# Attention and scan on one core: where the weighted sums stand in the slot order, and how the input norm is computed

## The chip, the cores and the metric

The kernel runs on one core of a Trainium2 chip. The metric is device time in microseconds; before the change it is 6852.26 us, the median of 3 runs (6847.03 to 6880.9). All arithmetic is float32.

## The reference, cut to what matters

Two layers are added to `x` (8 batches, 1024 tokens, 512 channels) one after the other. The change touches the first, an attention whose weights are modulated by a style vector per batch:

```python
x = x * s1[:, None, :]                       # s1 = cond[:, :512]
mu = jnp.mean(x, axis=-1, keepdims=True)
var = jnp.mean(jnp.square(x - mu), axis=-1, keepdims=True)
x = (x - mu) * jax.lax.rsqrt(var + EPS_IN)   # the input norm
q = heads(einsum('bsh,oh->bso', x, q_weight) * q_dc)      # 16 heads of 32
k = heads(einsum('bsh,oh->bso', x, k_weight) * k_dc)
v_flat = einsum('bsh,oh->bso', x, v_weight) * v_dc * s2
attn = softmax(einsum('bhqd,bhkd->bhqk', q, k) * scale)
out = einsum('bhqk,bhkd->bhqd', attn, heads(v_flat))      # the weighted sums
out = einsum('bsh,oh->bso', out, w_weight) * w_dc
skip = einsum('bsh,oh->bso', v_flat, u_weight) * u_dc
return out + skip
```

The factors `q_dc` to `u_dc` ("demodulation") are one over the root of sums of squared weights times squared styles. The second layer, a gated scan over the tokens, follows in the same program and isn't changed.

## The kernel before, in words

The order of instructions on every engine is the order in which the program writes them; no scheduler moves them. The attention is a loop over **slots**. A block is a batch `b` and a group `o` of four heads (128 channels); a block has 16 slots: 8 query tiles of 128 tokens (`q`), each with two pairs of heads (`pair`). So there are 32 blocks and 512 slots, and the loop index `n` counts slots (L302).

A slot does the following for its two heads, and overlaps it with the slot before:

- `scores` (L226): four matmuls on quarters of the array, 32 rows each, into two score tiles of two PSUM banks each. Two such tiles exist, so the next slot's scores need this slot's exps to be done.
- VectorE takes the row maxima from PSUM (L327), ScalarE the exps with their sums (L336), VectorE the reciprocals (L341, L354), and GpSimd (POOL) scales the probabilities in place (L356).
- The probabilities of the slot before are flipped by `flip` (L241, eight transposes a head on TensorE). Each flip of four tiles is copied out of PSUM into `pT`, by ScalarE (L333, L347) and VectorE (L338, L346).
- Two slots (four heads) share one `pT`. `weigh` (L248) multiplies it with the transposed values `vt`, in columns of 32, into the PSUM tile `av`. Before the change this runs in two halves of 16 matmuls, at the ends of the two slots that follow (L352), and VectorE copies `av` to `aT` one slot later (L319).

Work of other blocks is fed in as **background**: `background` (L275) is a generator of pieces, each some instructions long. A slot runs some of its pieces between the first and the second flips (L342) and the rest at its end (L357). `PIECES` (L298) gives the number of pieces of a block by `o`, spread evenly. Pieces are: `project` (L150), chains of four matmuls of 512 columns that make q, k and v of the next block, two matmuls to a piece, with an evacuation in the second piece by ScalarE (L165, L169, L174), then two pieces of four transposes of v (L182); `out_u` and `out_w`, chains with evacuation by VectorE (L198, L214); and `norm` of the next batch, whose first half is done in `o=2` and whose second in `o=3`. All of these chains share one PSUM buffer, `ps_m` (L95).

`norm` (L113) works on channels by tokens: GpSimd multiplies by the style (L116), a chain with a matrix of 1/512 gives the mean in every partition, VectorE subtracts it (L121), GpSimd squares (L127), a second chain gives the variance, ScalarE takes the root (L132), VectorE the reciprocal (L136), GpSimd multiplies (L140). A half is 512 tokens, 4 tiles of 128 channels. `load_x` (L56) fetches a half from `xT`, ahead of its use.

Before the loop, in program order: both halves of batch 0 are loaded, the five weight matrices are loaded (two buffers) and squared, and small matmuls make the demodulation factors (L64 to L87); then both halves are normed, the first weights fetched, and block 0 projected.

Of the kernel before, what the change touches and what calls it, by code (L numbers as in the profile page):

```python
# [28 lines left out]


@with_exitstack
def modulated_attention(ctx, tc, const, x1_d, xu_d, S, xT, wT, ident, sT):

# [7 lines left out]
    nc = tc.nc  # L41
    HW = S // 2
    KT = S // P
# [7 lines left out]
    ones = const.tile([P, P], F32, name="ones_h")  # L51
    nc.vector.memset(ones, 1.0 / H)
    dc = const.tile([P, 5, KH, B], F32, name="dc")
    xp = ctx.enter_context(tc.tile_pool(name="xh", bufs=3))

    def load_x(b, hf):  # L56
        xh = xp.tile([P, KH, HW], F32, name="xh")
        nc.sync.dma_start(
            out=xh, in_=xT[b, :, hf * HW : (hf + 1) * HW].rearrange("(k p) t -> p k t", p=P)
        )  # L60
        return xh

    xh_now = [load_x(0, 0), load_x(0, 1)]
    with tc.tile_pool(name="w0", bufs=2) as wp, tc.tile_pool(name="ps_d", bufs=2, space=PSUM) as ps_d:  # L64
# [27 lines left out]
    small = ctx.enter_context(tc.tile_pool(name="small", bufs=6))  # L92
    ps_s = ctx.enter_context(tc.tile_pool(name="ps_s", bufs=2, space=PSUM))
    ps_t = ctx.enter_context(tc.tile_pool(name="ps_t", bufs=2, space=PSUM))
    ps_m = ctx.enter_context(tc.tile_pool(name="ps_m", bufs=1, space=PSUM))  # L95
    ps_v = ctx.enter_context(tc.tile_pool(name="ps_v", bufs=1, space=PSUM))

    def half(hf):
# [4 lines left out]
    def chain(pieces, evac):  # L103

        ps = ps_m.tile([P, HW], F32, tag="mm", name="mm_ps")
        for k, (w, x) in enumerate(pieces):
            nc.tensor.matmul(ps, w, x, start=(k == 0), stop=(k == KH - 1))  # L107
            if k == 1:
                yield
        evac(ps)  # L110
        yield

    def norm(xh, b):  # L113

        for k in range(KH):
            nc.gpsimd.tensor_scalar(xh[:, k], xh[:, k], sT[:, k, b : b + 1], 1.0, ALU.mult, ALU.mult)  # L116
        yield

        def center(ps):
            for k in range(KH):  # L120
                nc.vector.tensor_sub(xh[:, k], xh[:, k], ps)  # L121

        yield from chain([(ones, xh[:, k]) for k in range(KH)], center)
        sq = []
        for k in range(KH):
            sq.append(ring.tile([P, HW], F32, tag="sq", bufs=4, name="sq"))
            nc.gpsimd.tensor_mul(sq[k], xh[:, k], xh[:, k])  # L127
        yield
        rstd = ring.tile([P, HW], F32, tag="rstd", bufs=1, name="rstd")
        yield from chain(  # L130
            [(ones, sq[k]) for k in range(KH)],
            lambda ps: nc.scalar.activation(rstd, ps, AF.Sqrt, bias=eps),  # L132
        )
        for k in range(KH):
            c = slice(k * P, (k + 1) * P)
            nc.vector.reciprocal(rstd[:, c], rstd[:, c])  # L136
            if k % 2 == 1:
                yield
        for k in range(KH):
            nc.gpsimd.tensor_mul(xh[:, k], xh[:, k], rstd)  # L140
        yield

    def load_w(name, o):
# [101 lines left out]
            nc.tensor.transpose(ps[:, j], pr[:, c0 : c0 + P], ident)  # L245
        return ps

    def weigh(av, pT, vt, part):  # L248
        for kt in range(4 * part, 4 * part + 4):
            for i in range(4):  # L250
                r = slice(i * HD, (i + 1) * HD)
                nc.tensor.matmul(  # L252
                    av[r], vt[:, kt, r], pT[:, i, kt], start=(kt == 0), stop=(kt == KT - 1),
                    skip_group_check=True,
                )

    blocks = [(b, o) for b in range(B) for o in range(KH)]
    sts = {bo: {} for bo in blocks}
    slots = [(bo, q, pair) for bo in blocks for q in range(NQ) for pair in range(2)]
# [15 lines left out]
    def background(n):  # L275

        nonlocal xh_now
        b, o = blocks[n]
        if o == 2 and b + 1 < B:
            xh_next.append(load_x(b + 1, 0))  # L280
        if o < KH - 1:
            yield from project(wts[n + 1], xh_now, b, o + 1, sts[b, o + 1])
            if o == 2 and b + 1 < B:
                xh_next.append(load_x(b + 1, 1))
                yield from norm(xh_next[0], b + 1)
        elif b + 1 < B:
            yield from norm(xh_next[1], b + 1)
# [9 lines left out]
    xh_next = []  # L297
    PIECES = {0: 22, 1: 22, 2: 23, 3: 39}  # L298
    probs = None
    flipped = {}  # L300
    bg, ran = iter(()), 0
    for n in range(len(slots) + 4):  # L302
        bo, q, pair = slots[n] if n < len(slots) else (None, None, None)
        if n % SB == 0:
            for _ in bg:
# [5 lines left out]
            ran += due  # L311


        m = (n - 5) // 2
        if n % 2 == 1 and m >= 0:
            mbo, mq, _ = slots[2 * m]
            if mq == 0:
                sts[mbo]["a"] = ring.tile([P, S], F32, tag="aT", bufs=6, name="aT")
            nc.vector.tensor_copy(sts[mbo]["a"][:, mq * P : (mq + 1) * P], flipped.pop(m)[1])  # L319
        fresh = None  # L320
        if bo is not None:
            s_ps = scores(sts[bo], q, pair)
# [4 lines left out]
                nc.vector.tensor_reduce(nmax[i], s_ps[i], AX.X, ALU.max, negate=True)  # L327
        if probs is not None:
            if (n - 1) % 2 == 0:
                flipped[(n - 1) // 2] = [two.tile([P, 4, KT, P], F32, name="pT"), None]  # L330
            pT = flipped[(n - 1) // 2][0][:, 2 * ((n - 1) % 2) : 2 * ((n - 1) % 2) + 2]
# [12 lines left out]
        if probs is not None:  # L344
            t_ps = [flip(probs[1], g) for g in range(2)]
            nc.vector.tensor_copy(pT[:, 1, 4:8], t_ps[1])  # L346
            nc.scalar.copy(pT[:, 1, 0:4], t_ps[0])  # L347
# [478 lines left out]
def network(ctx: ExitStack, tc: tile.TileContext, S, ins, out):  # L826
    nc = tc.nc
    const = ctx.enter_context(tc.tile_pool(name="const", bufs=1))
# [6 lines left out]
    nc.sync.dma_start(out=sT, in_=ins["condT"].rearrange("(k p) b -> p k b", p=P))  # L835
    with tc.manual_schedule():
        modulated_attention(
            tc, const, x1_d, xu_d, S, ins["xT"], {n: ins[f"w{n}T"] for n in "qkvwu"}, ident, sT
        )
# [68 lines left out]
```

## Time and profile before

| | |
|---|---|
| median of 3 runs | 6852.26 us (6847.03 to 6880.9) |
| the profiled execution | 6840.93 us |
| its span, first to last instruction | 6838.9 us |
| mean granted clock of TensorE | 0.947 |
| first scores of the attention | 117.1 us |
| last scores of the attention | about 3695 us |
| TensorE busy, of the stretch 0 to 4000 us | 3662 us |
| VectorE, ScalarE, GpSimd busy there | 2358, 2096, 1334 us |

Times in the profile are microseconds from the start of the span. "PE" is TensorE's matmuls and "PEld" its weight loads, which overlap them; DVE is VectorE, ACT is ScalarE, POOL is GpSimd, SP the engine that issues the DMAs. A row of a timeline gives the start, the length, the engine, the source line, the operation, and the tile written with those read. A float32 matmul other than a transpose shows as two records. The attention is regular: blocks with the same `o` take the same time in batches 1 to 6.

### The profile page before, as it was taken

To read this page: it belongs to the slowest core of one execution; us is meant where nothing else is said; L and a number is where in the kernel's file an instruction comes from. 1 tells how busy PE (TensorE), PEld (TensorE's weight loads), DVE (VectorE), ACT (ScalarE), POOL (GpSimd) and SP (SyncE) were. 2 spreads that over 40 slices of the span, in tenths; PEclk is the share of its full clock that TensorE was granted. 3 is DMA by queue.
4 is the path that set the end of the run, shared out by engine and by line. 5 is a ranking of instruction groups with operands and counts; after the bars stand their busy time and mean duration, and the time that the engine had idled before them with its cause. 6 is when DMAs were issued, how large, how long until landed. Compare 5 with 4: busy or idle time off the path is not lost.

```text
span 6838.9 us, 113125 instructions
## 1 busy us (share of the span) xinstructions
PE 6072.8 (89%) x42960; PEld 3291.8 (48%) x42960; DVE 4499.3 (66%) x6851; ACT 3919.7 (57%) x6713; POOL 1333.6 (20%) x1220
## 2 busy tenths in 40 slices
PE   7889989899899898998997788888888888888887
PEld 4555545555555455555554444444434444444443
DVE  2656656656566566565664677777777777777776
ACT  3555545545555455555553566666666666666665
POOL 2343333423433334234332000000000000000000
PEclk9999999999999999999999898999889998899898
DMA  2011111111111111111112777778777787777776
GB/s 67 18 32 50 46 43 41 30 55 44 33 49 46 43 44 29 57 43 37 44 34 75 192 202 202 199 197 208 202 196 204 199 209 200 196 203 196 202 205 174
DMA packets 493518, 777.47 MB, mean 114 GB/s; under 512 B 197008, under 2 KB 295448, under 8 KB 492976
## 3 DMA queue, kind: packets, MB, share of 16 engines
q1 hardware_dynamic: 492976, 770.22, 43.3%
q8 instruction: 342, 5.60, 0.3%
q14 instruction: 200, 1.64, 0.1%
HBM read 659.40 MB, written 83.89 MB: 109 GB/s over the span
## 4 chain that ended last, share of the span: by engine, by line
PE 64%; DVE 17%; DMA 7%; ACT 4%; issue 4%; SPq 2%; POOL 1%; DVEq 0%; ACTq 0%; POOLq 0%
PE mm_ps L107 17%; PE t_ps L245 12%; PE s_ps L235 7%; PE av L252 7%; DVE h L755 7%; PE o_ps L701 5%; PE g_ps L663 4%; DMA xb<-xd 4%; PE y_ps L742 3%; PE in_ps L508 3%; DVE nmax L327 2%; PE p_ps L539 2%; SPq L724 1%; ACT xb L731 1%; DVE gate L678 1%
## 5 line engine op out<-in xcount | busy, mean ns | idle before, releaser
L755 DVE CUSTOM_DVE_ANT_0 h<-h,xb,lim 128x1024 f32<-128x1024 f32 x1024 | 1374.1, 1342 | 587.5 <-ACT xb L731 335.2
L327 DVE TENSOR_REDUCE nmax<-s_ps 128x1 f32<-128x1024 f32 x1024 | 1205.0, 1218 | 767.6 <-PE s_ps L238 763.7
L356 POOL TENSOR_SCALAR pr<-pr,rinv 128x1024 f32<-128x1024 f32 x1024 | 1148.2, 1122 | 2279.5 <-PE t_ps L245 1515.8
L245 PEld LDWEIGHTS t_ps<-ident,pr 128*128 128x128 f32 x8192 | 904.7, 141 | 868.1 <-issue 609.0
L245 PE MATMUL t_ps<-ident,pr 128*128 128x128 f32 x8192 | 1156.7, 280 | 170.3 <-DVE pT L338 124.8
L336 ACT ACTIVATE pr<-s_ps,nmax 128x1024 f32<-128x1024 f32 x1024 | 1141.5, 1115 | 83.9 <-DVE nmax L327 60.3
L731 ACT ACTIVATE xb<-xb,ws 128x1024 f32<-128x1024 f32 x1024 | 1154.0, 1140 | 30.8 <-DMA xb<-xd 30.8
L333 ACT COPY pT<-t_ps 128x512 f32<-128x512 f32 x512 | 300.1, 586 | 1313.6 <-PE t_ps L245 1313.6
L742 PE MATMUL y_ps<-h,yw 128*32 128x512 f32 x4096 | 647.1, 720 | 8.0 <-DVE h L755 8.0
L346 DVE COPY pT<-t_ps 128x512 f32<-128x512 f32 x512 | 353.2, 690 | 399.9 <-PE t_ps L245 397.7
L235 PE MATMUL s_ps<-kT,qT 32*128 32x512 f32 x2048 | 579.7, 640 | 0.0
L238 PE MATMUL s_ps<-k,q 32*128 32x512 f32 x2048 | 577.1, 640 | 0.0
L252 PE MATMUL av<-pT,vt 128*32 128x128 f32 x16384 | 559.2, 278 | 0.4 <-DVE aT L319 0.4
L508 PE MATMUL in_ps<-x,win 128*128 128x256 f32 x2048 | 543.2, 412 | 3.6 <-DMA x<-x_d 2.8
L508 PEld LDWEIGHTS in_ps<-x,win 128*128 128x128 f32 x2048 | 401.2, 205 | 162.8 <-issue 59.2
L701 PE MATMUL o_ps<-wout,gT 128*128 128x512 f32 x1024 | 468.0, 600 | 0.5 <-ACT gT L689 0.5
L252 PEld LDWEIGHTS av<-pT,vt 128*32 128x32 f32 x16384 | 420.1, 110 | 88.0 <-issue 86.6
L663 PE MATMUL g_ps<-win,x1t 128*128 128x512 f32 x1024 | 460.5, 592 | 0.4 <-ACT x1t L658 0.4
L527 DVE SCALAR_TENSOR_TENSOR xc<-xr,cw,xc 128x256 f32<-128x256 f32 x768 | 370.7, 483 | 26.7 <-ACT xc L520 8.4
L338 DVE COPY pT<-t_ps 128x512 f32<-128x512 f32 x512 | 348.4, 680 | 2.6 <-PE t_ps L245 2.6
L347 ACT COPY pT<-t_ps 128x512 f32<-128x512 f32 x512 | 297.4, 581 | 82.2 <-PE t_ps L245 82.2
L684 PE MATMUL gt_ps<-ident,gate 128*128 128x128 f32 x512 | 108.8, 350 | 243.7 <-DVE gate L678 243.7
(128 smaller groups left out, 6381.5 us busy)
## 6 DMA issues: line engine op xcount, KB each, us to landing
xb<-xd SPq DMA_DIRECT2D x2048, 256.0 KB
xd<-xt SPq DMA_DIRECT2D x64, 512.0 KB
xh<-in_xT SPq DMA_DIRECT2D x16, 1024.0 KB
q<-qT SPq DMA_DIRECT2D x128, 128.0 KB
xr<-in_xT SPq DMA_DIRECT2D x64, 256.0 KB
xu_d<-xr SPq DMA_DIRECT2D x64, 256.0 KB
xr<-xu_d SPq DMA_DIRECT2D x64, 256.0 KB
x_d<-xr SPq DMA_DIRECT2D x64, 256.0 KB
```

The costliest lines, as they stand in the source:

```text
L107: nc.tensor.matmul(ps, w, x, start=(k == 0), stop=(k == KH - 1))
L235: nc.tensor.matmul(s_ps[i][:, 0:HW], st["q"][r, qc], st["k"][r, 0:HW], start=True, stop=True)
L245: nc.tensor.transpose(ps[:, j], pr[:, c0 : c0 + P], ident)
L252: nc.tensor.matmul(av[r], vt[:, kt, r], pT[:, i, kt], start=(kt == 0), stop=(kt == KT - 1), skip_group_check=True,)
L327: nc.vector.tensor_reduce(nmax[i], s_ps[i], AX.X, ALU.max, negate=True)
L336: nc.scalar.activation(fresh[i], s_ps[i], AF.Exp, bias=nmax[i], accum_out=rsum[i])
L356: nc.gpsimd.tensor_scalar(fresh[i], fresh[i], rinv[i], 1.0, ALU.mult, ALU.mult)
L508: nc.tensor.matmul(ps, win_sb[:, kk, k * P : (k + 1) * P], st["x1"][:, kk].rearrange("p b t -> p (b t)"), start=(kk == 0), stop=False,)
L701: nc.tensor.matmul(ps, st["gT", i][:, k, :], wout_sb[:, k, :], start=False, stop=(k == KI - 1), skip_group_check=True,)
L731: nc.scalar.mul(xbs[n], xbs[n], sts[c]["ws"][:, t : t + 1])
L742: nc.tensor.matmul(st["y", i][32 * r : 32 * r + 32, hf * 512 : (hf + 1) * 512], yws[i][:, 4 * q + r, :], hs[4 * g + r][:, hf * 512 : (hf + ...
L755: nc.vector._custom_dve(dve_ops.TENSOR_ADD_SAT, out=h, in0=last["h"], in1=xbs.pop(n), s0=lim[:, 0, t : t + 1], s1=lim[:, 1, t : t + 1],)
```

## The change

It has three parts. First, `weigh` runs whole, 32 matmuls, in every second slot (odd `n`), ahead of that slot's scores; the copy of `av` to `aT` follows at once, and the loop has two slots fewer at its end. Second, `norm` works on tokens by channels: `x` is loaded by tokens, with the style spread over 128 partitions by the DMA; GpSimd multiplies by the style, VectorE takes mean and variance with `bn_stats` and `bn_aggr`, ScalarE the root of the 128x4 variances, GpSimd scales and shifts, and TensorE transposes the result into `xh`, four 128x128 tiles into a PSUM bank at a time, evacuated in turn by ScalarE and VectorE. A half is now 10 pieces where it was 9, and `PIECES` follows. Third, batch 0 is normed before the demodulation, whose matmuls now use the shared PSUM buffer.

```diff
     def load_x(b, hf):
+        xq = tok.tile([P, 4, H], F32, name="xq")
+        nc.sync.dma_start(
+            out=xq, in_=x[b, hf * HW : (hf + 1) * HW].rearrange("(j p) c -> p j c", p=P)
+        )
+        sr = tok.tile([P, H], F32, name="sr")
+        nc.sync.dma_start(out=sr, in_=cond[b, 0:H].unsqueeze(0).to_broadcast([P, H]))
+        return xq, sr
+
+    def norm(xs, put):
+        xq, sr = xs
         xh = xp.tile([P, KH, HW], F32, name="xh")
-        nc.sync.dma_start(
-            out=xh, in_=xT[b, :, hf * HW : (hf + 1) * HW].rearrange("(k p) t -> p k t", p=P)
-        )
-        return xh
-
-    xh_now = [load_x(0, 0), load_x(0, 1)]
+        put(xh)
+        mv = small.tile([P, 4, 2], F32, name="mv")
+        rs = small.tile([P, 4, 2], F32, name="rs")
+        for j in range(4):
+            nc.gpsimd.tensor_mul(xq[:, j], xq[:, j], sr)
+            if j % 2 == 1:
+                yield
+        for j in range(4):
+            stat = small.tile([P, 6], F32, name="stat")
+            nc.vector.bn_stats(stat, xq[:, j])
+            nc.vector.bn_aggr(mv[:, j], stat)
+            if j % 2 == 1:
+                yield
+        nc.scalar.activation(rs[:, :, 0], mv[:, :, 1], AF.Sqrt, bias=eps)
+        nc.vector.reciprocal(rs[:, :, 0], rs[:, :, 0])
+        nc.vector.scalar_tensor_tensor(
+            rs[:, :, 1], mv[:, :, 0], -1.0, rs[:, :, 0], ALU.mult, ALU.mult
+        )
+        yield
+        for j in range(4):
+            nc.gpsimd.tensor_scalar(xq[:, j], xq[:, j], rs[:, j, 0:1], rs[:, j, 1:2], ALU.mult, ALU.add)
+        yield
+        for k in range(KH):
+            ps = ps_m.tile([P, 4, P], F32, tag="mm", name="mm_ps")
+            for j in range(4):
+                nc.tensor.transpose(ps[:, j], xq[:, j, k * P : (k + 1) * P], ident)
+            if k % 2 == 0:
+                nc.scalar.copy(xh[:, k], ps.rearrange("p j t -> p (j t)"))
+            else:
+                nc.vector.tensor_copy(xh[:, k], ps.rearrange("p j t -> p (j t)"))
+            yield
+
+    xh_now = []
+    first = [load_x(0, 0), load_x(0, 1)]
+    for xs in first:
+        for _ in norm(xs, xh_now.append):
+            pass
...
-            d_ps = ps_d.tile([P, KH, B], F32, name="d_ps")
+            d_ps = ps_m.tile([P, KH, B], F32, tag="mm", name="mm_ps")
...
-    for hf in range(2):
-        for _ in norm(xh_now[hf], 0):
-            pass
...
-    def weigh(av, pT, vt, part):
-        for kt in range(4 * part, 4 * part + 4):
+    def weigh(av, pT, vt):
+        for kt in range(KT):
...
-    PIECES = {0: 22, 1: 22, 2: 23, 3: 39}
+    PIECES = {0: 22, 1: 22, 2: 24, 3: 40}
...
-    for n in range(len(slots) + 4):
+    for n in range(len(slots) + 2):
...
-        m = (n - 5) // 2
+        m = (n - 3) // 2
         if n % 2 == 1 and m >= 0:
             mbo, mq, _ = slots[2 * m]
+            av = ps_v.tile([P, P], F32, name="av")
+            weigh(av, flipped.pop(m), sts[mbo]["vt"])
             if mq == 0:
                 sts[mbo]["a"] = ring.tile([P, S], F32, tag="aT", bufs=6, name="aT")
-            nc.vector.tensor_copy(sts[mbo]["a"][:, mq * P : (mq + 1) * P], flipped.pop(m)[1])
+            nc.vector.tensor_copy(sts[mbo]["a"][:, mq * P : (mq + 1) * P], av)
...
-        m = (n - 3) // 2
-        if 0 <= m < len(slots) // 2:
-            if n % 2 == 1:
-                flipped[m][1] = ps_v.tile([P, P], F32, name="av")
-            weigh(flipped[m][1], flipped[m][0], sts[slots[2 * m][0]]["vt"], (n + 1) % 2)
```

The old `norm` goes out whole, with the matrix of 1/512. In `background` the loads of the next batch stay where they were; only the tiles that they hand over are others.

More of the change, by code (lines that the diff above doesn't have):

```diff
@@ L31, in modulated_attention @@
 @with_exitstack
-def modulated_attention(ctx, tc, const, x1_d, xu_d, S, xT, wT, ident, sT):
+def modulated_attention(ctx, tc, const, x1_d, xu_d, S, x, xT, cond, wT, ident, sT):
     nc = tc.nc
@@ L50, in modulated_attention @@
     nc.vector.memset(eps, EPS)
-    ones = const.tile([P, P], F32, name="ones_h")
-    nc.vector.memset(ones, 1.0 / H)
     dc = const.tile([P, 5, KH, B], F32, name="dc")
     xp = ctx.enter_context(tc.tile_pool(name="xh", bufs=3))
+    tok = ctx.enter_context(tc.tile_pool(name="tok", bufs=2))
+    small = ctx.enter_context(tc.tile_pool(name="small", bufs=6))
+    ps_m = ctx.enter_context(tc.tile_pool(name="ps_m", bufs=1, space=PSUM))
     def load_x(b, hf):
-        xh = xp.tile([P, KH, HW], F32, name="xh")
-        nc.sync.dma_start(
-            out=xh, in_=xT[b, :, hf * HW : (hf + 1) * HW].rearrange("(k p) t -> p k t", p=P)
-        )
-        return xh
@@ L63, in modulated_attention @@
-    xh_now = [load_x(0, 0), load_x(0, 1)]
-    with tc.tile_pool(name="w0", bufs=2) as wp, tc.tile_pool(name="ps_d", bufs=2, space=PSUM) as ps_d:
+        xq = tok.tile([P, 4, H], F32, name="xq")
[7 more added lines that the diff above has]
+        xq, sr = xs
+        xh = xp.tile([P, KH, HW], F32, name="xh")
+        put(xh)
[15 more added lines that the diff above has]
+            rs[:, :, 1], mv[:, :, 0], -1.0, rs[:, :, 0], ALU.mult, ALU.mult
+        )
+        yield
[11 more added lines that the diff above has]
+            yield
@@ L65, in modulated_attention @@
+    xh_now = []
[3 more added lines that the diff above has]
+            pass
+    with tc.tile_pool(name="w0", bufs=2) as wp:
         s2T = wp.tile([P, 2 * KH, B], F32, name="s2T")
@@ L91, in modulated_attention @@
     pp = ctx.enter_context(tc.tile_pool(name="pp", bufs=4))
-    small = ctx.enter_context(tc.tile_pool(name="small", bufs=6))
     ps_s = ctx.enter_context(tc.tile_pool(name="ps_s", bufs=2, space=PSUM))
     ps_t = ctx.enter_context(tc.tile_pool(name="ps_t", bufs=2, space=PSUM))
-    ps_m = ctx.enter_context(tc.tile_pool(name="ps_m", bufs=1, space=PSUM))
     ps_v = ctx.enter_context(tc.tile_pool(name="ps_v", bufs=1, space=PSUM))
@@ L110, in chain @@
         evac(ps)
[L111 to L132, printed above, removed]
-        )
[L134 to L140, printed above, removed]
         yield
@@ L279, in background @@
         if o == 2 and b + 1 < B:
-            xh_next.append(load_x(b + 1, 0))
+            todo.append(load_x(b + 1, 0))
         if o < KH - 1:
@@ L283, in background @@
             if o == 2 and b + 1 < B:
-                xh_next.append(load_x(b + 1, 1))
-                yield from norm(xh_next[0], b + 1)
+                todo.append(load_x(b + 1, 1))
+                yield from norm(todo.pop(0), xh_next.append)
         elif b + 1 < B:
-            yield from norm(xh_next[1], b + 1)
+            yield from norm(todo.pop(0), xh_next.append)
             xh_now = list(xh_next)
@@ L295, in background @@
             yield from out_u(b, [sts[b, k]["v"] for k in range(KH)])
-    xh_next = []
-    PIECES = {0: 22, 1: 22, 2: 23, 3: 39}
+    todo, xh_next = [], []
+    PIECES = {0: 22, 1: 22, 2: 24, 3: 40}
     probs = None
@@ L329, in modulated_attention @@
             if (n - 1) % 2 == 0:
-                flipped[(n - 1) // 2] = [two.tile([P, 4, KT, P], F32, name="pT"), None]
-            pT = flipped[(n - 1) // 2][0][:, 2 * ((n - 1) % 2) : 2 * ((n - 1) % 2) + 2]
+                flipped[(n - 1) // 2] = two.tile([P, 4, KT, P], F32, name="pT")
+            pT = flipped[(n - 1) // 2][:, 2 * ((n - 1) % 2) : 2 * ((n - 1) % 2) + 2]
             t_ps = [flip(probs[0], g) for g in range(2)]
@@ L837, in network @@
         modulated_attention(
-            tc, const, x1_d, xu_d, S, ins["xT"], {n: ins[f"w{n}T"] for n in "qkvwu"}, ident, sT
+            tc, const, x1_d, xu_d, S, ins["x"], ins["xT"], ins["cond"], {n: ins[f"w{n}T"] for n in "qkvwu"}, ident, sT
         )
@@ L869 @@
     arrays = {
+        "x": np.asarray(x),
         "xT": np.asarray(x).transpose(0, 2, 1),
```

## The prediction

> **What bounds the kernel now.** First the page: the parts with the engines and with the chain that ended last.
>
> ```profile
> PE 6072.8 (89%) x42960; PEld 3291.8 (48%) x42960; DVE 4499.3 (66%) x6851; ACT 3919.7 (57%) x6713; POOL 1333.6 (20%) x1220
> PE 64%; DVE 17%; DMA 7%; ACT 4%; issue 4%; SPq 2%; POOL 1%; DVEq 0%; ACTq 0%; POOLq 0%
> ```
>
> The matmuls of the attention (the first 3,730 us) carry the chain, so I need the order on TensorE, not the busy sums. The timeline of one slot gives it (start, length, engine; the bracket is the idle time before and what ended it):
>
> ```profile
> 1500.37 0.19 PEld L235 LDWEIGHTS s_ps<-kT,qT 32*128 32x128 f32 x2 [0.20 <-issue]
> 1501.44 0.86 PEld L245 LDWEIGHTS t_ps<-ident,pr 128*128 128x128 f32 x8 [0.76 <-issue]
> ...
> 1505.03 0.19 ACT L336 ACTIVATION_READ_ACCUMULATOR pr<-s_ps,nmax 128x1 f32 x1
> 1505.16 0.81 PEld L252 LDWEIGHTS av<-pT,vt 128*32 128x32 f32 x32 [0.17 <-issue]
> 1505.69 0.58 ACT L347 COPY pT<-t_ps 128x512 f32<-128x512 f32 x1
> 1506.17 0.30 PEld L107 LDWEIGHTS mm_ps<-xh,w_k 128*128 128x128 f32 x2 [0.20 <-issue]
> 1508.08 0.19 PEld L235 LDWEIGHTS s_ps<-kT,qT 32*128 32x128 f32 x2 [0.76 <-issue]
> ```
>
> The slot reads: scores S 1.07 us; first flips F0 0.83; background piece B1 1.40; second flips F1 with what follows 1.49, so that the sums W start at S+4.79; W 1.01, ending at 5.80; background B2 1.91. With B2 a slot is 7.71, without it 5.80. ScalarE ends the second exp at S+4.75, then evacuates B1 if due (0.68), then makes the last copy of the flips (L347) at S+4.74 to 5.32, or here, behind an evacuation, to 5.90.
>
> The first slots have no sums yet, so they show how slots run once W is gone:
>
> ```profile
> 126.83 0.23 PEld L235 LDWEIGHTS s_ps<-kT,qT 32*128 32x128 f32 x2 [0.17 <-ACT pr L336]
> 132.34 0.30 PEld L107 LDWEIGHTS mm_ps<-xh,w_v 128*128 128x128 f32 x2 [0.86 <-ACT kT L169]
> ```
>
> Scores then wait for the exp of the slot before; a B2 that begins a chain just after a B1 that ended one waits 0.86 us for the single mm_ps buffer.
>
> Stretches of 10 us around the norm (TensorE, its weight loads, DVE, ACT, POOL busy; then the clock):
>
> ```profile
> 1310.00:1320.00 10.00, 7.16 (x88) 4.36 (x76) 7.89 (x14) 6.69 (x11) 2.81 (x4) 1.00 0.00 0
> 1320.00:1330.00 10.00, 6.19 (x62) 3.63 (x61) 6.37 (x10) 5.84 (x11) 10.00 (x11) 1.00 0.01 2
> 1330.00:1340.00 10.00, 7.09 (x67) 4.05 (x66) 6.37 (x11) 3.16 (x7) 6.62 (x7) 1.00 0.01 2
> 1340.00:1350.00 10.00, 10.00 (x108) 5.59 (x107) 3.78 (x6) 5.66 (x10) 3.36 (x3) 1.00 0.00 0
> 1350.00:1360.00 10.00, 4.91 (x52) 3.36 (x48) 8.05 (x13) 5.30 (x9) 6.70 (x6) 0.76 0.01 2
> ```
>
> Here TensorE idles about 15 us per batch. Starts of scores give block times (16 slots): 103.0 for o=0 and 1, 104.7 for o=2, 143.1 for o=3, the same in batches 1 to 6.
>
> [...] a weight load waits 0.76 us from a 512-column chain into scores, 0.24 from chain to chain; 0.17 before W, 0.20 behind it. [...] the trace has 0.76 at 1350 to 1360, after stalls in which only flips ran. [...] a switch loads a table; the trace agrees, at 1.28 us a load [...].
>
> **The sums moved.** Two times 16 matmuls become 32 in one place: 1.01 + 1.01 becomes about 1.83 (the tail has 32 beside each other, 64 records in 1.9). Each pair of slots loses one entry (0.17) and one exit (0.20), and where an even slot has B2, W comes behind it, at the price of the drain that scores paid there (0.76 - 0.24 = 0.52). But W now comes at the start of an odd slot, directly behind F1 of the even slot, whose last copy (L347) it reads from its fourth matmul on; in the old place it read the slot before. So:
> - even slot without B2: W resumes at S+5.37, slot 7.15; with an evacuation ahead of L347 7.73.
> - even slot with B2 (it hides L347): 4.62 + 1.40 + 0.5 drain + 1.83 = 8.36; if B2 waits 0.89 for mm_ps, which W used to hide: 9.25.
> - odd slot without B2: scores follow F1, at the end of the second exp, 4.85. With B2 6.53; if that waits 7.42.
>
> Queued behind the waiting W are the next scores, and behind them reductions, exps and POOL. The aT copy sits ahead of the reductions on DVE but ends (0.29) under the 1.07 of scores: nothing.
>
> A block o=0 or 1 (22 pieces, B2 in slots 0, 2, 5, 8, 10, 13), pairs after minus before: (0,1) 13.21-13.51 = -0.30; (2,3) 14.10-13.51 = +0.59; (4,5) 14.57-13.51 = +1.06; (6,7) 12.58-11.60 = +0.98; (8,9), v's transposes, 12.80-12.20 = +0.60; (10,11) -0.30; (12,13) 13.68-13.51 = +0.17; (14,15) +0.40. Sum +3.2; x14 = +45. In batch 0 the pieces end early: +4.1 twice.
>
> **The norm.** Removed per half: 8 chain matmuls of 0.854 (6.8 us of TensorE), 4 subtractions 0.68, 4 reciprocals 0.914, POOL 4 each of 0.70, 1.04 and 1.27. Added: 16 transposes (4 take about 0.43 of issue), four evacuations 0.58 (ACT) or 0.69 (DVE), 4 bn_stats at 0.69 and 4 bn_aggr at 0.21 (rows of the second stage[...]), POOL 4 at 1.27 and 4 at 0.70. The two table loads per half stay. No row shows POOL's scaling with two columns; bounds 0.56 (half of the 1.12 of L356) and 1.27, I take 0.70. The x load grows by 0.25 MB of broadcast styles; DMA share is 0.1 to 0.2: nothing.
>
> Walk of o=2 (24 pieces): slots 0 to 7, all even ones with B2, 54.6; 8 and 9 12.7; then slot 10 7.1, 11 4.9, 12 9.45 (sqrt and its table load at S+5.6 to 7.05 delay L347 to 7.6, W waits), 13 6.1 (exp table reload), 14 7.5, 15 4.9. Sum 107.3 against 104.7: +2.6, x8 = +21.
> o=3 (40 pieces): slot 0 7.2 (POOL's four products, 5.1, push the first scaling of pr to 8.35, just in time), slot 1 4.9, slot 2 10.4 (the first transposes wait for POOL's four scalings, ready at S+6.1, almost 4 us of idle TensorE), slot 3 6.05: 28.5 against 39.0. Slots 4 to 15, by the prices above, 105.1 against 104.1. Sum -9.5, x7 = -66. Batch 7, without norm, +1.5.
>
> **The clock.** Before has one half-clock episode a batch, worth about 2.3 us (W 1.94 for 1.08, flips, one chain), inside the 143.1. After has two candidate stalls (o=2 slot 12, o=3 slot 2), none in my walk. I add one episode a batch, +16; none would be 0, two +32.
>
> **The start.** Before: demodulation ends at 51.3, the norm takes until 88.3 on the path, scores at 117.1. After: x at about 7.5 (SP issues x and styles ahead of w, so w lands some 0.5 MB later than 12.7, long before its turn); per half POOL 5.1, stats and roots 1.9, scalings 2.8, four transposes with evacuations 5.6; POOL's in-order halves end with scalings at 27.3, transposes at 33. ScalarE squares the weights only behind that, so d_ps starts at 34, takes 36.5 (the two w buffers gate it as before; d_ps in one PSUM buffer adds some 0.2 each, under the wait for w) to 70.5, w_q lands about 74, and 28.8 later scores start at 103: -14 (-8 to -18). The end loses two slots of sums: -1.
>
> Sum: 45 + 8 + 21 - 66 + 1.5 + 16 - 14 - 1 = +10 on a profiled 6840.9 us, of which the span is 6838.9. The median shown is 6852.3, 11 higher; I put the sum on it: **6862**.
>
> **Rivals.**
> A, faster: the newly exposed waits don't appear, because W's first matmuls and the reordered loads cover L347, or the mm_ps waits close. For: the order on TensorE really loses a drain in every pair. Against: 1505.69 for L347 lies behind 1505.16. Without these waits a block o=0 or 1 is 5.5 better (-88), the others about 2 each: about 6745; with half of it, 6805. 0.13.
> B, slower: ScalarE's loop becomes the bound of odd slots. It holds 0.59 + 2.34 + 0.19 + 0.58 + 0.68 = 4.4 of the 4.85 us that I give them, and scores there wait for the second exp; the early instance took 5.0. Some 165 odd slots have no B2. At 0.15 more each it adds 25 and passes the bound of 34 us together with my sum; at 0.4, 66: about 6920. For: the wait on L336 in the early slot. Against: that slot had unevenly started scores. 0.30 with all that lies above 6886.
> C, the norm's gain comes larger: POOL's scalings at 0.56, no clock episode, DVE free earlier: 6862 - 16 - 7 x 2 = 6832. Inside no change.
> D, the kernel is the same but for the start: gains and losses cancel otherwise: 6838. It lies inside no change too; C and D have 0.25 of its 0.57.
>
> **How the numbers follow.** About 0.5% (34 us) is what a measurement of this kernel can tell from no change. Faster (A) 0.13, within 0.57, slower (B, and two clock episodes with slow norm stalls) 0.30. The error of a pair, about 0.1 us over 256 pairs, is 26; the norm walk 3 a batch, 21; start 6. The range that leaves out 0.2 is 6815 to 6910: at the low end half of A, at the high end most of B.
>
> **What would show it.** Right: scores from slot to slot alternate near 7.15 or 8.36 and 4.85; L347 becomes the releaser of W in even slots without B2 (0.5 to 1.1 us each, some 64 of them in o=0 and 1); waits of mm_ps behind qT, kT, vT grow; block times about 106, 106, 107, 134; first scores near 103. Wrong: no wait of W on L347 (A); odd slots at 5.2 or more (B); block o=3 not under 138 (the norm still stalls); first scores not before 110; two stretches of low clock a batch.

## The result, and the profile after

The changed kernel takes 6896.4 us (median of 13 runs, 6877.1 to 6916.9) where the kernel before took 6851.2 (13 runs, 6838.6 to 6880.9): a ratio of 1.0053, interval 1.0037 to 1.0068. It is slower by 45 us in the medians (0.66%) and by 0.53% in the ratio, just beyond the 0.5% that I called "no change". The forecast was +10, with a range that holds the result. The profiled execution took 6894.9 us, its span 6893.1, against 6840.9 and 6838.9: +54.

The page of the changed kernel, with the parts on the engines and on the chain that ended last:

```profile
PE 6051.7 (88%) x42960; PEld 3345.8 (49%) x42960; DVE 4490.3 (65%) x6914; ACT 3925.7 (57%) x6744; POOL 1272.4 (18%) x1156
PE 54%; DVE 19%; ACT 11%; DMA 9%; issue 4%; SPq 2%; POOL 0%; DVEq 0%; ACTq 0%; POOLq 0%
```

TensorE has 21 us less work than before and the kernel is longer: work is not what grew. The chain has moved in part from TensorE (54%, it was 64%) to ScalarE (11%, it was 4%). The timeline at the end of an even slot without B2 (block o=1 of batch 3; its scores start at 1622.67) and the first scores of the odd slot behind it say where (start, length, engine, line; the bracket is the idle time before and what ended it):

```profile
1627.43 0.19 ACT L348 ACTIVATION_READ_ACCUMULATOR pr<-s_ps,nmax 128x1 f32 x1
1627.52 0.57 ACT L359 COPY pT<-t_ps 128x512 f32<-128x512 f32 x1
1627.55 0.15 PEld L265 LDWEIGHTS av<-pT,vt 128*32 128x32 f32 x6 [0.17 <-issue]
...
1628.14 1.67 PEld L265 LDWEIGHTS av<-pT,vt 128*32 128x32 f32 x58 [0.44 <-ACT pT L359]
...
1630.01 0.19 PEld L248 LDWEIGHTS s_ps<-kT,qT 32*128 32x128 f32 x2 [0.20 <-issue]
```

The sums stop after six records, three matmuls, until ScalarE's last copy (L359) is there. The copy starts 0.03 us ahead of the sums and can't start earlier, because ScalarE has just ended the second exp. Before, the half of the sums at the end of an even slot read copies made two slots earlier, the half at the end of an odd slot those of the slot before, and nothing stopped. The waits of TensorE's weight loads from 100 to 3700 us (total, times, longest) show how often:

```profile
PEld av L265 <- ACT pT L359: 60.7, 91, 2.0
PEld mm_ps L150 <- ACT kT L182: 35.3, 40, 1.6
PEld mm_ps L195 <- ACT vT L187: 15.3, 17, 1.6
```

Before, no wait of the sums for a copy is listed, 2.5 us in 2 places for kT, and 1.6 in 1 for the v transposes. All three answer to terms of the prediction: the exposed copy, and the single mm_ps buffer that the sums no longer hide.

By starts of scores, after minus before in the two profiled executions:

| term | predicted | measured |
|---|---|---|
| first scores (start) | -14 | -6.1 (111.06 for 117.13) |
| o=0 and 1, batches 1 to 7 | +45 | +53.3 |
| o=0 and 1, batch 0 | +8 | +20.2 |
| o=2, and the half-clock term | +21 and +16 | +37.5 |
| o=3, batches 0 to 6 | -66 | -59.3 |
| o=3, batch 7 | +1.5 | +3.2 |
| behind the last scores | -1 | +5.3 |
| sum | +10 | +54.2 |

### The profile page after: what moved, and what is told of

It is laid out like the page before. It is cut to its first block, busy times and chain, and to the rows that moved or that the text cites. A ratio compares the mean times of both kernels' runs of the same rounds, so it can differ in the third digit from the quotient of the medians.

```text
span 6893.1 us, 113052 instructions
## 1 busy us (share of the span) xinstructions
PE 6051.7 (88%) x42960; PEld 3345.8 (49%) x42960; DVE 4490.3 (65%) x6914; ACT 3925.7 (57%) x6744; POOL 1272.4 (18%) x1156
## 4 chain that ended last, share of the span: by engine, by line
PE 54%; DVE 19%; ACT 11%; DMA 9%; issue 4%; SPq 2%; POOL 0%; DVEq 0%; ACTq 0%; POOLq 0%
PE mm_ps L150 12%; PE s_ps L248 8%; PE av L265 7%; PE t_ps L258 7%; ACT pr L348 6%; DVE h L762 6%; DVE nmax L339 5%; DMA xb<-xd 5%; PE o_ps L708 4%; PE g_ps L670 4%; PE y_ps L749 3%; PE in_ps L515 3%; DMA x<-x_d 2%; SPq L731 2%; PE p_ps L546 2%
## 5 line engine op out<-in xcount | busy, mean ns | idle before, releaser
L248 PE MATMUL s_ps<-kT,qT 32*128 32x512 f32 x2048 | 608.2, 643 | 1.3 <-ACT pr L348 1.3
L265 PEld LDWEIGHTS av<-pT,vt 128*32 128x32 f32 x16384 | 462.1, 112 | 176.1 <-issue 111.8
L331 DVE COPY aT<-av 128x128 f32<-128x128 f32 x256 | 74.7, 292 | 571.8 <-PE av L265 570.6
L359 ACT COPY pT<-t_ps 128x512 f32<-128x512 f32 x512 | 297.1, 580 | 68.0 <-PE t_ps L258 68.0
```

The lines of the kernel that those rows point to most:

```text
L248: nc.tensor.matmul(s_ps[i][:, 0:HW], st["q"][r, qc], st["k"][r, 0:HW], start=True, stop=True)
L265: nc.tensor.matmul(av[r], vt[:, kt, r], pT[:, i, kt], start=(kt == 0), stop=(kt == KT - 1), skip_group_check=True,)
```

## The experiments

Each was measured beside the kernel before, which took 6859.1, 6858.6 and 6866.6 us in the three sessions. "Loop" means first to last scores: 3577.4 us before, 3632.4 after. Times of blocks come from one profiled execution of each kernel.

**The parts one at a time.** The first kernel is the one before with the sums' move alone:

```diff
+            av = ps_v.tile([P, P], F32, name="av")
+            weigh(av, flipped.pop(m), sts[mbo]["vt"])
...
-            weigh(flipped[m][1], flipped[m][0], sts[slots[2 * m][0]]["vt"], (n + 1) % 2)
```

> The kernel before with the first part of the change alone: sums whole at the start of odd slots, norm and start as before. Theory 1 (the sums' new place costs in the slots: waits for the last copy of the flips and for mm_ps that the old place hid): blocks o=0 and 1 of 106.7 us as in the changed kernel against 103.0, batch 0's with more, so about +72 from these blocks and +1 to 2 in each of the others: 6925 to 6940, a ratio of 1.011 to 1.013. Rival (the loss came with the norm and its half-clock episodes): within 20 us of before.

Measured: 6930.1 us, ratio 1.0102 (1.0082 to 1.0123); the loop +87.5. Blocks o=0 and 1 take 106.7 to 106.9 as in the changed kernel, and the sums wait for the last copy for 74.1 us in 102 places. o=2 takes some 114 (+9.5) and o=3 136 (-7.0): the two together lose 2.6 a batch, with the split unlike what I expected. The move alone is a loss, and its price in the undisturbed blocks doesn't depend on the norm.

The second kernel is the changed one with the sums back in halves at the ends of the slots, so that the norm and the start are all that is new:

```diff
-            weigh(av, flipped.pop(m), sts[mbo]["vt"])
...
+            weigh(flipped[m][1], flipped[m][0], sts[slots[2 * m][0]]["vt"], (n + 1) % 2)
```

> The changed kernel with the sums put back as two halves at the ends of the slots: norm by tokens and first norm ahead of demodulation remain. Theory 1: o=0 and 1 return to 103.0, o=3 stays near 134, o=2 at 106 to 107, first scores at 111: about 7 us less per batch with a norm and 6 at the start, so about -55: 6797, a ratio of 0.992. Rival: the norm's own stalls and half-clock episodes eat its gain, o=2 stays at 109 and the time is that of before within 15.

Measured: 6777.1 us, ratio 0.9877 (0.9859 to 0.9894), and once more in another session:

> The kernel with sums in halves and norm by tokens once more, on the same chip as the interleaved start, so that the two can be set beside each other: a ratio of 0.988 to before, first scores at 110.

6788.9, ratio 0.989 (0.9874 to 0.9906). Blocks o=0 and 1 are back at 103.0, first scores at 110.1, the loop at 3521.4 (3522.5 again). So the norm by tokens gains 56 us of loop (o=2 +18.1, o=3 -74.5), and with it in place the sums' move costs 111: 53.1 in o=0 and 1 of batches 1 to 7, 20.2 in batch 0, 19.3 in o=2, 18.4 in o=3 (of the 20.2, about 10 come in this execution only, as is shown below).

**Is the cost the exposed copy?** Here the sums are whole too, but run at the end of the odd slot, one place later, with the copy of `av` at the head of the slot that follows:

```diff
-        m = (n - 3) // 2
-        if n % 2 == 1 and m >= 0:
+        m = (n - 4) // 2
+        if n % 2 == 0 and m >= 0:
...
             nc.scalar.copy(pT[:, 1, 0:4], t_ps[0])
+        m = (n - 3) // 2
+        if n % 2 == 1 and 0 <= m < len(slots) // 2:
+            av = ps_v.tile([P, P], F32, name="av")
+            weigh(av, flipped.pop(m), sts[slots[2 * m][0]]["vt"])
```

> The changed kernel with the 32 matmuls still in one place, but at the end of the odd slot, behind its second flips, and the copy of av in the next slot: they read flips of the slots before, so the last copy is long made. Theory 1 (the wait for the last copy is the loss): even slots without B2 fall from 7.3 to 4.85, odd ones rise from 4.8 to 6.6, blocks o=0 and 1 at 102.8 against 106.7: about -70, 6825. Rival (the waits for mm_ps and the scores' wait for exp are the loss): blocks stay at 105 or more, 6880 or more.

Measured: 6820.1 us, ratio 0.9938 (0.9923 to 0.9953); the loop 3553.5, 79 us shorter than after (10 of it in batch 0, by what is shown below of the clock there). The timeline of TensorE's weight loads at the end of an odd slot, the last of o=1 in batch 3, and then ScalarE's row for the last copy of the same slot:

```profile
1655.91 0.89 PEld L258 LDWEIGHTS t_ps<-ident,pr 128*128 128x128 f32 x7 [0.29 <-issue]
1656.97 1.69 PEld L265 LDWEIGHTS av<-pT,vt 128*32 128x32 f32 x64 [0.17 <-issue]
1658.85 0.19 PEld L248 LDWEIGHTS s_ps<-kT,qT 32*128 32x128 f32 x2 [0.20 <-issue]
```

```profile
1656.93 0.57 ACT L357 COPY pT<-t_ps 128x512 f32<-128x512 f32 x1
```

The sums run 64 records without a stop although the copy of this slot is as late as ever (1656.93 to 1657.50), since they read the slots before. In this kernel no wait of the sums for a copy is listed. Merging 16 and 16 into 32 is thus not what costs; reading what was flipped immediately before is. The waits for the single mm_ps buffer can hardly be it either: kT (29.4 us for 35.3 in the changed kernel) and the v transposes (15.4 for 15.3) still wait here, and the blocks are short all the same. Merging gains nothing either: o=0 and 1 take 103.3 or a little more, against 103.0 with halves, though each pair saves one wait ahead of the sums (0.17 us in the timeline above) and one behind them (0.20). o=2 here takes some 110, longer than with halves, and I didn't settle why.

**The order of the start.** The changed kernel with the first norm behind the demodulation, as before:

```diff
-    for xs in first:
-        for _ in norm(xs, xh_now.append):
-            pass
...
+    for xs in first:
+        for _ in norm(xs, xh_now.append):
+            pass
     fetch_w(0)
```

> The changed kernel with the first norm again behind the demodulation. Theory 1 (ahead of it, the norm's chain through POOL, VectorE and TensorE delays ScalarE's squares and so the demodulation, which waits for DMA anyway): POOL's products run under the demodulation, the demodulation ends near 52 again, the norm takes 19 more, first scores near 100 against 111.1: 11 us less, about 6885. Rival (the norm by tokens is on the path in either order): first scores at 111 or later, time unchanged.

Measured: 6902.1 us, ratio 1.0064 (1.0048 to 1.008); first scores 114.7 us, against 111.1. The gain that I expected didn't come. VectorE's timeline of this kernel (the last row of the demodulation; the first statistics and the last evacuation of the first half; the first statistics of the second):

```profile
55.49 0.19 DVE L127 TENSOR_TENSOR dc<-dc,sT 128x32 f32<-128x32 f32 x1
55.60 0.69 DVE L79 BATCH_NORM_STATS2 stat<-xq 128x6 f32<-128x512 f32 x1
...
68.89 0.69 DVE L99 COPY xh<-mm_ps 128x512 f32<-128x512 f32 x1 [3.00 <-PE mm_ps L95]
69.50 0.68 DVE L79 BATCH_NORM_STATS2 stat<-xq 128x6 f32<-128x512 f32 x1
```

The first half's product had been there since 14.0 us, but in program order the first half's statistics stand behind the demodulation's last steps and start at 55.60, the second half's behind the first half's evacuations, at 69.50. First scores are 3.6 us earlier with the norm first, the times of the two kernels can't be told apart, and each order leaves one of two chains uncovered. A third order, on top of the norm with sums in halves, takes the products and statistics of both halves and the root of the first ahead, the root of the second behind the first groups of the demodulation's matmuls, and puts the transposes between the later groups; the demodulation has a PSUM pool of its own again:

```diff
-    for xs in first:
-        for _ in norm(xs, xh_now.append):
-            pass
+    gens = [norm(xs, xh_now.append) for xs in first]
+    for p in (2, 2):
+        for h in range(2):
+            run(h, p)
+    run(0, 2)
...
+                if n == 0 and o == 1:
+                    run(1, 2)
+                elif n in (1, 2):
+                    run(n - 1, 1)
```

Here `run(h, count)` advances the norm of half `h` by `count` pieces.

> The kernel with sums in halves and norm by tokens (6777 when it ran first), with the start interleaved: products, statistics and roots of both halves first, the transposes between the groups of the demodulation's matmuls, whose PSUM pool is its own again. Theory 1 (both orders of the first norm cost because ScalarE, VectorE and TensorE take norm and demodulation one after the other): the demodulation ends near 57, first scores near 90 against 110, the rest unchanged: about 6757. Rival (the loads of w gate the start in any order): first scores at 105 or later, 6772 or more.

Measured: 6763.0 us, ratio 0.9856 (0.9837 to 0.9874), and again

> The kernel with sums in halves, norm by tokens and interleaved start once more, on the same chip: a ratio of 0.9856 to before within its interval, first scores at 92.5.

6769.3, ratio 0.9854 (0.9834 to 0.9874). First scores at 92.2 to 92.5, 19 us ahead of the changed kernel. Its TensorE, from the second run's timeline:

```profile
33.27 1.09 PE L95 MATMUL mm_ps<-ident,xq 128*128 128x128 f32 x4
34.40 1.87 PE L127 MATMUL d_ps<-s2T,w 128*128 128x8 f32 x8
...
61.93 5.14 PE L161 MATMUL mm_ps<-xh,w_q 128*128 128x512 f32 x8 [3.42 <-DMA w_q<-in_wqT]
```

The transposes stand between the demodulation's matmuls, and the first projection starts at 61.9 instead of 79.3. What they fill are not gaps of TensorE, though. Stretches over the demodulation (TensorE, weight loads, VectorE, ScalarE, POOL busy), in the changed kernel and then in this one:

```profile
39.50:75.90 36.40, 34.83 (x160) 34.50 (x160) 0.77 (x5) 7.46 (x4) 0.00 (x0) 1.00 0.27 87
```

```profile
17.36:58.51 41.15, 41.08 (x192) 40.18 (x192) 5.78 (x17) 9.98 (x9) 7.66 (x10) 1.00 0.22 77
```

The demodulation's 160 records alone keep TensorE busy for 34.8 of 36.4 us, so it is its own matmuls that set its length, and not the loads of the weights, by which the prediction and the expectation for the late norm had it gated. The transposes lengthen it by some 5 us; what is won is that POOL's, VectorE's and ScalarE's steps of the norm run beside it. This is the fastest kernel of the study, faster than both.

**Does the half clock cost much?** In the profile the changed kernel has more of it: adding up twice the missing clock over stretches of 10 us from 100 to 3600 us gives 102 us at half clock, against 48 before. Two edits put dummy matmuls on TensorE, two of 512 columns into a PSUM tile that nothing reads; what is computed stays. The first puts them where the background has run out:

```diff
-            next(bg, None)
+            if next(bg, "end") == "end":
+                ps = ps_m.tile([P, HW], F32, tag="mm", name="mm_ps")
+                for k in range(2):
+                    nc.tensor.matmul(ps, ident, xh_now[0][:, k], start=(k == 0), stop=(k == 1))
```

> The changed kernel with two matmuls of 512 columns (identity by xh, never read) in each slot whose background has run out; they fit into the wait for the copy of the first flips. They add work, nothing is left out. Theory 1 (the 20 us that batch 0's blocks o=0 and 1 lost against 8 foreseen are half clock in slots where only flips, scores and sums run; with the first norm late those slots took 7.3 and 4.8 instead of 8.9 and 4.8, from another start time): the pairs stay at 12.1, batch 0's first two blocks at about 100 and 104 instead of 105.2 and 109.3, about 10 us less than the changed kernel, 6886. Rival (these slots are long for another reason): the pairs stay at 13.7, 6896.

Measured: 6915.2 us, ratio 1.0076 (1.0059 to 1.0092). Batch 0's blocks fall to 100.4 and 104.4, as expected. But batch 7's o=3 (up to the last scores) grows to 117.4 from 108.0, because its later slots take up to two dummy chains each. o=3 of the other batches is mostly at 137, but the kernel with the norm late, which has no dummies, shows 137 in five of them too. And what seemed to be confirmed was not due to the edit, as the next kernel shows. The second edit puts the same matmuls into six pieces of the norm that give TensorE nothing to do, in o=2 and o=3 alone:

```diff
             if j % 2 == 1:
+                warm()
                 yield
...
+        warm()
         yield
```

It was made on the changed kernel and on the fastest one:

> The changed kernel with two matmuls of 512 columns (identity by q of the block, never read) in each of the six pieces of a norm that give TensorE nothing to do. Work is added, none left out. Theory 1 (the norm's blocks o=2 came out at 109.4 instead of 107.3 because stretches with flips alone halve the clock): half clock in these stretches goes (102 us of it between 100 and 3600 in the changed kernel, 48 before), o=2 falls to about 107, o=3 to about 133: about 15 to 25 less than the changed kernel, 6875. Rival (the norm's waits for POOL and the sqrt set the length, not the clock): o=2 stays at 109 or rises by the added matmuls' 1.7 us each where they don't fit, 6896 or more.

> The same matmuls in the kernel with sums in halves, norm by tokens and interleaved start (6763 when it ran first), where half clock is 51 us between 100 and 3600. Theory 1: at most half of that can come back, o=2 at 105 and o=3 at 131.7: about 10 less, 6753. Rival: no gain, 6763 or more by what the added matmuls cost.

Measured: 6904.8 us on the changed kernel, ratio 1.0053 (1.0036 to 1.007), where the changed kernel's own is the same 1.0053; and 6791.3 on the fastest, ratio 0.9887 (0.9869 to 0.9904), 22 slower than without. Time at half clock fell from 102 us to 44, and on the fastest kernel to 7 from 51 in its first run and 58 in the second. So with the dummies there is less half clock; that stretches with flips alone halve it, as the first of the two expectations has it, was my estimate, and no run shows what does. The second pair is the clean case: nearly all of the half clock is gone, and beside the second run o=2 gains 5 us in eight blocks and o=3 loses 28 in seven. So the half clock is no lever in this way: keeping the clock up with dummies costs more TensorE time than the clock returns. It does have a price where it falls on a matmul that the path waits for, as slot 12 of o=2 shows. The changed kernel, in batch 3, where the granted clock is 0.50 from 1788.46 to 1791.87:

```profile
1786.97 0.15 PEld L265 LDWEIGHTS av<-pT,vt 128*32 128x32 f32 x6 [0.17 <-issue]
1787.05 1.28 ACT L83 ACT_TABLE_LOAD   x1
1788.35 0.30 ACT L83 ACTIVATE rs<-mv,eps_h 128x4 f32<-128x4 f32 x1
1788.55 0.56 ACT L359 COPY pT<-t_ps 128x512 f32<-128x512 f32 x1
1789.16 2.97 PEld L265 LDWEIGHTS av<-pT,vt 128*32 128x32 f32 x58 [2.04 <-ACT pT L359]
```

The same place with the dummies in the norm:

```profile
1785.79 1.67 PEld L275 LDWEIGHTS av<-pT,vt 128*32 128x32 f32 x58 [0.32 <-ACT pT L369]
```

The wait of 2.04 us for the copy behind the table load was in my walk; the sums at 2.97 for 1.67 were not in that slot but in the separate half-clock term. With the dummies the sums take the 1.67 us that the changed kernel's took at a granted clock of 1.00 (the row at 1628.14), and the slot takes 9.2 instead of 10.5, but slot 10 grows by 1.2 with the dummy in it.

The kernel with dummies in the norm alone also tells what happened in batch 0. Its instructions up to the end of o=1 of batch 0 are those of the changed kernel, and yet those blocks take 100.4 and 104.4 there against 105.2 and 109.3. The stretches from 180 to 200 us (TensorE, weight loads, VectorE, ScalarE, POOL busy; then the clock), the changed kernel first, then the one with dummies:

```profile
180.00:190.00 10.00, 8.41 (x98) 5.57 (x97) 4.83 (x9) 3.87 (x8) 3.05 (x4) 0.83 0.01 2
190.00:200.00 10.00, 8.35 (x99) 6.04 (x96) 5.13 (x8) 3.83 (x7) 3.21 (x3) 0.83 0.01 2
```

```profile
180.00:190.00 10.00, 7.81 (x98) 5.03 (x90) 6.47 (x10) 5.06 (x9) 3.38 (x3) 1.00 0.01 2
190.00:200.00 10.00, 7.81 (x103) 5.04 (x104) 5.74 (x12) 5.13 (x11) 3.88 (x4) 1.00 0.01 2
```

The same instructions, two outcomes: about 10 us of the profiled +54 belong to that execution and not to the order of instructions. The kernels with the norm late and with dummies behind the background also show 100.4 and 104.4, so the first of them, which changed nothing in these blocks, already took the ground from under the second. The trace of the changed kernel shows what lies between them. Its clock is half in six stretches of 3.41 us in these two blocks, one in each slow pair, starting at 180.79, 194.44 and 208.09 us in o=0 and at 290.01, 303.67 and 317.32 in o=1; the stretches around the first two (the clock is the third number from the end):

```profile
180.79:184.20 3.41, 3.41 (x62) 2.97 (x55) 0.24 (x2) 0.00 (x0) 1.12 (x1) 0.50 0.02 5
184.20:194.44 10.24, 7.26 (x62) 4.25 (x62) 7.52 (x13) 6.79 (x12) 3.37 (x3) 1.00 0.00 0
194.44:197.85 3.41, 3.41 (x62) 2.98 (x54) 0.16 (x3) 0.00 (x0) 1.12 (x1) 0.50 0.02 5
```

In a block they start 13.65 us apart, which is 4.0 times 3.41 and the length of the slow pairs of slots without background, 13.7 us (8.9 and 4.8); the pairs of the other execution take 12.1, which is 3.5 times. So pairs that once fall in step with the half clock would stay in step: an estimate of mine from these figures and from the grid of 3.413 us that is shown at the end. Half of six times 3.41 is 10.2 us, which accounts for the difference of 9.8. The kernel with dummies in the norm has none between 100 and 315 us. What no run varies is why one execution falls in step and another doesn't.

## Why the prediction was right, and where it was off

The forecast was the likeliest case of no change, at +10; what came is +45 in the medians and +54 in the profile. That is inside the range, but 6896.4 lies above the 6886 from which the prediction counted "slower", to which it gave 0.30. The main mechanism held: the exposed copy and the waits for mm_ps are where they were forecast. Still all seven rows of the table came out worse than written, one of them by half a microsecond, and their sum was too low by 44. Two of the signs that the prediction gave for being wrong appeared: first scores not before 110 (111.06), and more than one stretch of low clock a batch (three of 3.4 us in batches 3 to 6, where before has one of 6.8). So the place of the cost was foreseen, and its total stayed in the range by the width of the range. Point by point:

- **The slots.** 7.15 for an even slot without B2, 8.36 and 9.25 with it, 4.85 and 6.53 for odd ones were predicted; measured are 7.3, 8.5, 9.4, 4.8 and 6.5. For o=1 of batch 3 the eight pairs are 13.35, 14.16, 14.73, 12.60, 12.85, 13.27, 13.85 and 12.02, each 0.02 to 0.17 above its predicted value. The term is +3.8 a block instead of +3.2, +8 us over 14 blocks. The small shortfall is in the wait and the length of the sums: they resume at S+5.47, where I had S+5.37, and the slot ends another 0.09 later. What the prediction calls a drain is in the traces a wait of weight loads: behind a B2 those of the sums wait 0.76 us (at 1479.79, 1494.74 and 1508.92 in the changed kernel), from chain to chain 0.24. What TensorE does in it they don't show.
- **Rival A** (no exposed waits) is refuted by 60.7 us of them, and by what came back once the copy was covered. The last copy of the slot, which starts 0.53 us behind the sums in the timeline before (1505.69 and 1505.16), was the line to read, and it was read rightly.
- **Rival B** (ScalarE bounds the odd slots at 5.0 to 5.2) is refuted: 4.8 throughout the undisturbed blocks. The result lies on B's side without B's cause.
- **Batch 0** was predicted at +8, measured at +20.2 in this execution and +10.4 in a kernel whose instructions up to there are the same. The price of the order was right; I had not allowed for a half clock in the pairs without background. How often it occurs in the runs without a profile isn't known.
- **The norm.** o=2 with the half-clock term is +37.5 for the predicted 37 (that a stall of TensorE brings half clock was my estimate from the one episode a batch before, in batch 2 from 1355.23 for 6.83 us). That is right in sum, and partly in its place: slots 12 and 14 of o=2 took 10.5 and 9.3 for the predicted 9.45 and 7.5, slot 13 5.1 for 6.1, with the half clock in both even ones. o=3 gave -59 of the predicted -66: slots 0 to 3 took 29.4 in batch 3 instead of 28.5 (the transposes wait for POOL's scalings as priced), and three of the batches took 135.2 to 136.2 where batch 3 took 134.2. The size of this term is good to some 10 us only: in the kernel with the norm late, whose loop is the same, o=3 gave -50.
- **The start** is the step with the largest relative miss: first scores at 111 instead of 103. The terms that were mis-sized: POOL's first product started at 8.95, behind the DMA that spreads the style, where I had 7.5; the second half's statistics stood on VectorE behind the first half's evacuations and began at 25.42, though their products were ready at 23.7; the transposes and their evacuations, which take turns on one PSUM buffer (waits of 0.67 to 0.79 us between the groups), ended just ahead of 39.5 where I had 33; and the first projection was slow. The timeline of the changed kernel:

```profile
37.53 1.12 PE L95 MATMUL mm_ps<-ident,xq 128*128 128x128 f32 x4 [0.68 <-ACT xh L97]
39.52 6.97 PE L120 MATMUL mm_ps<-s2T,w 128*128 128x8 f32 x32 [0.88 <-ACT w L115]
...
79.33 6.59 PE L150 MATMUL mm_ps<-xh,w_q 128*128 128x512 f32 x8 [3.47 <-DMA w_q<-in_wqT]
86.75 3.70 PE L150 MATMUL mm_ps<-xh,w_k 128*128 128x512 f32 x8 [0.83 <-ACT qT L178]
```

  The demodulation took its 36.4 us as predicted, though by TensorE's own work and not by the weight buffers, and only from 39.5 on instead of 34; w_q was there at 79.3 instead of 74; and 6.59 for 3.70 cost 2.9 more.
- **The end** behind the last scores was +5.3 instead of -1. It differs from kernel to kernel by more than that: 3142.9 us in the kernel with the sums alone, 3157.7 in the one with the sums one place later, 3144.3 before. Apart from the last sums the changed code isn't in it, and I read no cause into it.

So the sum was short because errors that I had taken as even to both sides (0.1 us a pair, 3 a batch, 6 for the start) lay on one side, and because some 10 us of half clock in batch 0 stood in no term. A walk over slots counts the waits that it sees; those that it missed here all added. Two readings of before were slightly off too: o=2 takes 104.6 us for the 104.7 that I had, o=3 143.3 for 143.1.

## What to carry to other kernels

Before work is merged or moved, ask which of its inputs is the youngest at the new place: the same 32 matmuls cost some 70 us more where they read a copy made in the moment before than one place later. Separate a change of several parts on the chip before judging it, since here a gain of some 56 us and a loss of some 100 stood behind a result that looks like nothing. Where two orders of a start each leave an engine idle, look for the third in which the short pieces of one stand between the matmul groups of the other; here it was worth 19 us.

## What the runs showed of the hardware

- Two executions of the same instructions, up to about 315 us, ran at a granted clock of 0.83 and of 1.00 between 180 and 200 us, with 10 us between them by the end of o=1 of batch 0. The start of the scores differs by 0.9 us; I had taken the half clock as fixed by the order of instructions.
- In all twelve traces the changes of the granted clock lie on one grid of 3.413 us (in the changed kernel and in the one before to within 0.005 us), and between 100 and 3600 us each stretch of half clock lasts one or two of its steps. In some kernels the batch fits this grid: it repeats after 453.9 to 454.1 us before (133 steps, batches 1 to 6), 457.2 to 457.5 in batches 3 to 6 of the changed kernel (134), 460.6 to 461.1 in batches 1 to 5 of the changed kernel with dummies in the norm (135). The kernel with the norm late has, with the changed kernel's loop, batches of 457.2 and of 460.6 to 461.2. So 3 us a batch can lie between executions of one code; what sets them isn't shown.
- The first projection took 6.59 us in the changed kernel, 6.00 with the norm late and 5.14 in the fastest kernel, where the next one takes 3.70. The clock records of these traces begin, with full clock, at 85.21, 88.20 and 64.89 us, in the middle of this chain; ahead of them there is no record, and the 1.00 that a view shows there says nothing. Counted at half clock up to the first record and at full clock behind it, the three chains come to 3.65, 3.67 and 3.66 us of full clock, which is an estimate from these figures and the length of the next chain. By this estimate the clock was half until the first record, in the changed kernel behind 36.4 us of small matmuls of 8 columns and a wait of 3.5. It comes out so without that wait too: in the kernel before, the norm's first chain follows the small matmuls at once:

```profile
44.32 6.99 PE L75 MATMUL d_ps<-s2T,w 128*128 128x8 f32 x32 [0.97 <-ACT w L70]
51.16 5.46 PE L107 MATMUL mm_ps<-xh,ones_h 128*128 128x512 f32 x8
59.24 3.67 PE L107 MATMUL mm_ps<-sq,ones_h 128*128 128x512 f32 x8 [2.62 <-POOL sq L127]
```

  The first record stands at 54.75 us there, and the chain from 51.16, 5.46 us long, comes to 3.67 in the same way. Whether the small matmuls would be shorter at full clock no run shows.
- POOL's scaling with two column values took 3.01 us for four tiles of 128x512, 0.75 each, and its product with the spread style 4.93, 1.23 each; the prediction had taken 0.70 and 1.27 from neighbouring rows.
